# A two-layer convolution kernel: the order of work and the buffers at the opening of its second layer

## The chip, the cores and the metric

The kernel runs on one core of a Trainium2 chip. The metric is the device time of one execution in microseconds (us); the time before is the median of three runs. The engines are named as in the profile: PE is TensorE (matrix products) and PEld its weight loads, DVE is VectorE, ACT is ScalarE, POOL is GpSimd, and SP is the queue that issues all of this kernel's transfers.

## The reference

Two bottleneck layers follow one another on an input x of 64 images, 1024 channels, 14 x 14 positions, all in float32.

```python
# layer 0: 1x1 conv 1024->256, 3x3 conv 256->256, 1x1 conv 256->1024, each with batch norm
out = relu(bn(conv(x, w1) + b1)); out = relu(bn(conv(out, w2) + b2)); out = bn(conv(out, w3) + b3)
x = relu(x + softplus(residual_scale) * out)

# layer 1: 1x1 conv, deformable 3x3 conv, 1x1 conv, each with group norm (32 groups, per image)
a = relu(gn(conv(x, w1b)))                    # 256 channels
om = conv(a, w_off, pad=1) + b_off            # 27 channels: 9 x-offsets, 9 y-offsets, 9 masks
sampled[k] = bilinear(a, grid + tap k + offset k) * sigmoid(mask k)
h2 = relu(gn(einsum(sampled, w2b)))           # over 256 channels x 9 taps
out = relu(gn(conv(h2, w3b)) + x)
```

Batch norm needs statistics over all images, so no image can leave layer 0 before all have been through its third convolution. Group norm works on one image, so layer 1 goes through the images two at a time.

## The kernel before, in words

Layer 1 treats 32 pairs of images. A pair's stages are: the residual sum that ends layer 0 for it (`residual`, L212 on VectorE and a ReLU L224 on ScalarE for each of eight channel blocks); the first convolution (`first_conv`, L1072) with its statistics, norm and ReLU (`first_norm`, an object `gn1`); a transform of the result for the offset convolution (`transform`, L1136 on VectorE with an edge copy L1140 on GpSimd); the offset convolution (`offset_conv`, L1160), whose result is summed into the tile `off` by a bias on ScalarE (L1175) and eight additions on VectorE (L1176, L1177, L1187); sampling; the second convolution (`second_conv`, L1388, tile `pd`) with its norm `gn2`; the third (`third_conv`, L1500) with its norm.

Bilinear sampling is done as a matrix product (`sampling`, L1359): the transposed pixels `aT` of a pair times a matrix of weights. A weight is a product of a row factor and a column factor, each max(0, 1 - |distance|). `selection` writes `off` and the sigmoid of the masks to DRAM (tile `dm`, L1201 and L1202) and reads them back broadcast over rows (`wt` and `mk`, L1214). `factors` adds the grid (`distances`: L1224 on VectorE, then Abs and ReLU on ScalarE, L1225 and L1226), multiplies the row factor by the mask (L1231) and writes both factors to DRAM (`wd`, L1244). `spread_rows` and `spread_columns` read them back broadcast over 126 partitions: S (L1299) and X (L1321), each in three pieces for each of two sets of taps (e = 0: five taps, e = 1: four). `corners` multiplies S by X piece by piece (L1339). ScalarE then copies each sampled tile from PSUM to a buffer `sm` (L1367), 20 copies for a pair, and the second convolution reads `sm`.

To save space X lies in the buffer that later takes `sm` of the same set (`sample_buffer`, tags sm0 and sm1); the rest of the buffer sm1 takes the transform of the next pair. `transposes` makes `aT`; `lend` copies parts of it to other partitions by two transfers (L1275). `load(p)` fetches x of pair p (`load_x`, L195) and its third-convolution result of layer 0 (`load_h3`, L201).

TensorE's order is written out by hand as a list of steps (`put` places extra steps ahead of numbered ones, `weave` mixes two lists). `fill` is the opening: pairs 0, 1 and 2 go through their first stages before the loop over `slot(t)`, in which pair t is sampled and goes through its second convolution, while pair t+1 is prepared and pair t-1 finished. In the manual schedule only TensorE is bound to that order; instructions of other engines, transfers included, are placed by the scheduler, except those wrapped in `tc.keep_in_program_order`. [...]The same builder makes a second path (`FULL`) for larger offsets behind a branch.

Of the kernel before, what the change touches and what calls it, by code (L numbers as in the profile page):

```python
# [10 lines left out]
FP = mybir.dt.float32  # L11
AF = mybir.ActivationFunctionType
ALU = mybir.AluOpType
# [31 lines left out]
def kernel(  # L45
# [146 lines left out]

    def load_x(p):
        for i in range(2):
            nc.sync.dma_start(  # L195
                Y[p % 4][:, :, ts(i, HW)], x[2 * p + i].rearrange("(b p) q -> p b q", p=P)
            )

    def load_h3(p, r):
        for half in range(2):  # L200
            nc.sync.dma_start(  # L201
                r[:, ts(half, HB)].rearrange("p b q -> p (b q)"), h3[p][:, ts(half, HB * N2)]
            )
# [701 lines left out]
    def build_second_bottleneck(l1, path, run, early):  # L905
# [144 lines left out]
        def load(p):  # L1050
            start(p)
            load_x(p)
            load_h3(p, Z0)

# [163 lines left out]
        def factors(p):  # L1218
# [3 lines left out]
            def distances():  # L1222
                wt = q["wt"]
                tc.keep_in_program_order(nc.vector.tensor_tensor(wt, wt, base_sb, ALU.add))  # L1224
                nc.scalar.activation(wt, wt, AF.Abs)  # L1225
                nc.scalar.activation(wt, wt, AF.Relu, bias=1.0, scale=-1.0)  # L1226

# [40 lines left out]
        def lend(p):  # L1268

            aT = pairs[p]["aT"]  # L1270
            for j in range(1, NS - 1):
                m = (starts[0] + R - starts[j]) * W
                for k, q0, q1 in ((0, 0, m), (NS - 1, m, QR)):
                    first = (starts[j] - starts[k]) * W
                    nc.sync.dma_start(  # L1275
                        aT[q0:q1, :, :, j, :], aT[first + q0 : first + q1, :, :, k, :]
                    )
# [15 lines left out]
        def spread_rows(p, e):  # L1293

            q = pairs[p]
            k0, k1 = tapsets[e]
            S = one.tile([QR, wide * KT[e % 2]], FP, tag=f"S{e % 2}", name=f"S_{p}_{e}")
            for g, r0, piece in pieces(e):
                nc.sync.dma_start(  # L1299
                    S[:, piece],  # L1300
                    q["wd"][g][0, r0 : r0 + R, k0:k1, :]
                    .rearrange("r k n -> r (k n)")
                    .unsqueeze(1)
                    .to_broadcast([R, W, piece.stop - piece.start]),
                )
            q["S"][e] = S

        def spread_columns(p, e):
# [3 lines left out]
            n = wide * KT[e % 2]  # L1312
            if shared:
                t = sample_buffer(e, f"X_{p}_{e}")
                X = t[:QR, :n]
                if e == 1:
                    transformed[p + 1] = t[:, n:]
            else:
                X = one.tile([QR, n], FP, tag=f"X{e % 2}", name=f"X_{p}_{e}")
            for g, r0, piece in pieces(e):  # L1320
                nc.sync.dma_start(  # L1321
                    X[:, piece],
                    q["wd"][g][1, :, k0:k1, :]
# [3 lines left out]
                )  # L1327
            q["X"][e] = X

        def corners(p, e):  # L1330
# [5 lines left out]
            for g, r0, piece in pieces(e):  # L1336

                tc.keep_in_program_order(
                    nc.vector.tensor_tensor(S[:, piece], S[:, piece], X[:, piece], ALU.mult)  # L1339
                )  # L1340
# [282 lines left out]
        def slot(t):  # L1623
# [16 lines left out]
            for e in range(2, E):  # L1640
                sp[e - 2].append(lambda e=e: this and (spread_rows(t, e), spread_columns(t, e), corners(t, e)))
            d1 = part(front and not (early and t < 2), first_conv, t + 1)
            norm1, norm2, norm3 = (
                part(front, first_norm, t + 1),
                part(back, second_norm, t - 1),
# [16 lines left out]
            else:  # L1662
                extra = list(zip((3, 6, 8, 9, 10, 10, 10), norm2)) + list(zip((0, 2, 4, 4, 5, 5), norm1))
                extra = sorted(extra + [(9, w) for w in weights[1:]], key=lambda v: v[0])
# [13 lines left out]
            if ahead:  # L1678
                todo += [lambda: spread_rows(t + 1, 0), lambda: spread_columns(t + 1, 0)]
                todo += [lambda: spread_rows(t + 1, 1), lambda: lend(t + 1)]  # L1680
            if back:
# [4 lines left out]
            extra = [lambda: corners(t + 1, 0)] if t + 1 in ((1, NP - 1) if early else ()) else []  # L1686
            at = (12,)
            if t == NP - 1:

                extra, at = ends2[:-1], [len(pd[E - 1]) // 2 + n for n in (3, 5, 6, 6)]  # L1690
            todo += put(pd[E - 1], extra, at)
            if ahead:
                todo.append(lambda: spread_columns(t + 1, 1))
            for step in todo:
# [58 lines left out]
        def fill():  # L1753

            for p in range(3):
# [4 lines left out]
                first_conv(1),  # L1760
                first_norm(0) + [lambda: residual(2)] + offset_conv(0) + selection(0) + factors(0),
                (3, 6, 7, 7, 7, 7, 8) + (12,) * (MB * 3) + (12, 16, 16),
            )
            steps += [lambda: spread_rows(0, 0), lambda: spread_columns(0, 0), lambda: spread_rows(0, 1)]
            steps += transposes(0, nc.scalar.copy) + [lambda: lend(0), lambda: spread_columns(0, 1)]
            steps += put(
# [100 lines left out]
```

## Time and profile before

| | |
|---|---|
| median of three runs | 2965.86 us (2965.19 to 2966.86) |
| profiled execution | 2966.53 us, span 2964.7 us |
| PE busy | 2891.8 us, 98% of the span |
| DVE, ACT, POOL busy | 72%, 40%, 32% |
| mean granted PE clock | 0.993 |
| HBM traffic | 296.63 MB read, 116.76 MB written |

Layer 0's last product starts at about 968.5 us and layer 1's first at 970.0; pair 0's second convolution begins at 1041.34, and each later pair takes about 60.5 us. Busy time is the time of an engine's own instructions; a line of the chain of waits gives the start, the length and what the end of the program waited for at that time. In a timeline the brackets give the idle time ahead of an instruction and what ended it.

### The profile page before, as it was taken

How to read it: one execution, taken by the hardware profiler on the slowest of the kernel's cores; microseconds unless marked ns; L12 is line 12 of the kernel's file. 1: busy time of each engine (PE TensorE's matmuls, PEld its weight loads, DVE VectorE, ACT ScalarE, POOL GpSimd, SP SyncE). 2: the span in 40 equal slices, each digit the busy share in tenths (PEclk: the TensorE clock that was granted, in tenths of full speed). 3: DMA queues.
4: the chain of work that ended last, by engine and by line, in shares of the span. 5: the costliest groups of instructions: out<-in, count | busy, mean ns of one | idle time of the engine just before them, and what ended most of it. 6: DMA issues, size and time to landing. Idle time of an engine off the chain costs nothing.

```text
span 2964.7 us, 37198 instructions
## 1 busy us (share of the span) xinstructions
PE 2891.8 (98%) x11653; PEld 1829.8 (62%) x11653; DVE 2133.3 (72%) x5682; ACT 1180.9 (40%) x2504; POOL 934.5 (32%) x1003
## 2 busy tenths in 40 slices
PE   9999899989999899999999999999999999999997
PEld 5555555545555466666666666666666666666654
DVE  7877899997887656676666666676666666666655
ACT  0000222115555434444544454444544454444443
POOL 4621466654665111222122221222122221222121
PEclk9999999999999999999999999999999999999999
DMA  7665000005655425554556445644565445644531
GB/s 226 190 174 152 15 1 1 1 34 198 220 219 196 150 75 178 172 157 142 158 175 180 140 144 178 175 151 141 162 174 176 140 146 179 175 154 139 166 126 45
DMA packets 350419, 424.17 MB, mean 143 GB/s; under 512 B 27876, under 2 KB 292612, under 8 KB 349956
## 3 DMA queue, kind: packets, MB, share of 16 engines
q1 hardware_dynamic: 350212, 421.71, 46.1%
q8 instruction: 94, 1.54, 0.2%
q14 instruction: 113, 0.93, 0.1%
HBM read 296.63 MB, written 116.76 MB: 139 GB/s over the span
## 4 chain that ended last, share of the span: by engine, by line
PE 83%; DVE 10%; DMA 2%; ACT 2%; issue 1%; SPq 1%; POOL 0%; ACTq 0%; DVEq 0%; POOLq 0%
PE pd L1388 25%; PE d L1072 11%; PE sp L1359 11%; PE c L385 10%; PE c L766 9%; PE d L1500 8%; PE c L530 6%; DVE v L516 3%; PE om L1160 2%; DVE off L1187 1%; PE tr L1261 1%; DMA X<-wd 1%; PE c L731 1%; ACT sm L1367 1%; DVE V L1507 1%
## 5 line engine op out<-in xcount | busy, mean ns | idle before, releaser
L1388 PE MATMUL pd<-sm,w2b_sb 128*128 128x392 f32 x2304 | 791.7, 494 | 0.0
L1388 PEld LDWEIGHTS pd<-sm,w2b_sb 128*128 128x128 f32 x2304 | 424.6, 190 | 267.9
L1359 PE MATMUL sp<-S,aT 126*128 126x420 f32 (+3 forms) x1536 | 493.4, 418 | 22.6 <-ACT sm L1367 12.1
L1367 ACT COPY sm<-sp 128x336 f32<-128x336 f32 (+3 forms) x640 | 285.2, 451 | 265.0 <-PE sp L1359 236.4
L1072 PE MATMUL d<-h,w1b_sb 128*128 128x392 f32 x1024 | 357.2, 498 | 0.8 <-ACT h L224 0.8
L530 PE MATMUL c<-v,u_sb 128*128 128x392 f32 x1024 | 343.3, 498 | 10.9 <-DVE bn1sh L167 8.2
L530 PEld LDWEIGHTS c<-v,u_sb 128*128 128x128 f32 x1024 | 194.7, 192 | 159.4 <-DVE v L516 11.8
L1359 PEld LDWEIGHTS sp<-S,aT 126*128 126x128 f32 x1536 | 255.1, 190 | 46.8 <-ACT sm L1367 32.8
L1072 PEld LDWEIGHTS d<-h,w1b_sb 128*128 128x128 f32 x1024 | 189.3, 190 | 126.9 <-ACT h L224 3.0
L1582 ACT ACTIVATE z<-z,gn_0sh 128x196 f32<-128x196 f32 x504 | 182.7, 445 | 149.8 <-DVE gn_0sh L1034 134.0
L516 DVE TENSOR_TENSOR v<-t 128x392 f32<-128x392 f32 x256 | 193.1, 812 | 0.0
L1339 DVE TENSOR_TENSOR S<-S,X 126x840 f32<-126x840 f32 (+1 forms) x192 | 160.8, 888 | 38.0 <-DMA X<-wd 34.3
L1500 PE MATMUL d<-h,w3b_sb 128*128 128x196 f32 x744 | 180.4, 332 | 0.0
L1574 DVE SCALAR_TENSOR_TENSOR z<-z,gn_0sc,h 128x196 f32<-128x196 f32 x504 | 178.6, 417 | 0.0
L1018 POOL TENSOR_TENSOR gn_0sc<-gn_0sc,mhalf 128x16 f32<-128x16 f32 (+3 forms) x35 | 94.8, 2709 | 236.8 <-DVE gn_0sc L1017 227.6
L1500 PEld LDWEIGHTS d<-h,w3b_sb 128*128 128x128 f32 x744 | 133.0, 189 | 50.4 <-issue 19.4
L1512 POOL TENSOR_TENSOR E<-V,E 128x196 f32<-128x196 f32 x124 | 74.1, 597 | 281.8 <-DVE V L1507 281.8
L968 DVE BATCH_NORM_STATS2 gn_0st<-z 128x6 f32<-128x196 f32 x504 | 153.3, 349 | 4.2 <-ACT z L1551 0.9
L385 PE MATMUL c<-xc,w1a_sb 128*128 128x392 f32 x384 | 149.3, 497 | 5.8 <-DMA xc<-in_x_dram 5.8
L224 ACT ACTIVATE h<-h,bn3sh 128x392 f32<-128x392 f32 x256 | 140.7, 622 | 12.6 <-DVE h L212 12.6
L212 DVE SCALAR_TENSOR_TENSOR h<-h,bn3sc,h 128x392 f32<-128x392 f32 x256 | 140.7, 623 | 0.0
L718 DVE BATCH_NORM_STATS2 st<-o 128x6 f32<-128x392 f32 x256 | 127.9, 556 | 16.1 <-ACT o L749 9.5
(821 smaller groups left out, 4380.7 us busy)
## 6 DMA issues: line engine op xcount, KB each, us to landing
xc<-in_x_dram SPq DMA_DIRECT2D x128, 392.0 KB
h<-o SPq DMA_DIRECT2D x64, 784.0 KB
h<-in_x_dram SPq DMA_DIRECT2D x64, 784.0 KB
h<-h SPq DMA_DIRECT2D x64, 784.0 KB
out_dram<-z SPq DMA_DIRECT2D x126, 392.0 KB
X<-wd SPq DMA_DIRECT2D x64, 413.4 KB
S<-wd SPq DMA_DIRECT2D x64, 413.4 KB
S<-wd SPq DMA_DIRECT2D x64, 330.8 KB
```

Source lines behind the costliest of these rows:

```text
L385: nc.tensor.matmul(acc[m], a, b, start=(j == 0), stop=(j == HB - 1))
L516: nc.vector.tensor_tensor(v[:, u].rearrange("p (i y x) -> p i y x", y=7, x=7), cols[c][:, :, i : i + 13 : 2, :], cols[c][:, :, j : j + 13 ...
L530: nc.tensor.matmul(m[u], u_sb[:, c, u, k % 4, ts(o, P)], vts[k][c][:, u], start=(c == 0), stop=(c == MB - 1),)
L766: nc.tensor.matmul(planes(acc[m]), a, b, start=start, stop=True, skip_group_check=True)
L1072: nc.tensor.matmul(q["pt"][o], w1b_sb[:, c, ts(o, P)], q["y"][:, c, :], start=(c == 0), stop=(c == CB - 1),)
L1339: nc.vector.tensor_tensor(S[:, piece], S[:, piece], X[:, piece], ALU.mult)
L1359: nc.tensor.matmul(pt[:, i], q["aT"][:, i0 + i, c, starts.index(r0), :], q["S"][e][g, r0][:, :, i0 + i, :], start=(j == 0), stop=(j == len ...
L1367: nc.scalar.copy(dst, pt.rearrange("p i k n -> p k i n"))
L1388: nc.tensor.matmul(q["pd"][o], w2b_sb[:, c, k, ts(o, P)], q["sm"][e][:, c, k - k0].rearrange("p i q -> p (i q)"), start=(k == 0 and c == 0 ...
L1500: nc.tensor.matmul(bank[:, m % 2 if m < 6 else 1], a, b, start=(m < 6), stop=True, skip_group_check=True)
L1574: nc.vector.scalar_tensor_tensor(z[:, ts(i, HW)], z[:, ts(i, HW)], n.sc[:, b, i : i + 1], q["y"][:, o, ts(i, HW)], ALU.mult, ALU.add,)
L1582: nc.scalar.activation(z[:, ts(i, HW)], z[:, ts(i, HW)], AF.Relu, bias=n.sh[:, b, i : i + 1])
```

## The change

The change has these parts.

- In `fill`, the residual sum of pair 2 moves behind the offset convolution and `selection` of pair 0. The total of pair 1's statistics is pinned ahead of it.
- For pair 0, `distances` works on the column half and then the row half of `wt`, one after the other.
- X of pair 0, first set, goes to the two buffers of tag z (which the third convolution uses later), its last piece in the second of them, no longer to sm0.
- For pair 0 the pieces of S and X are issued in turn (S, X, S, X, ...), after the transposes and `lend`; the two spreading functions become generators.
- `load` (from slot 1 on) and `lend` keep their transfers in program order. In this build that moves pair 3's x and h3 loads behind pair 1's X, and pair 0's two `lend` transfers behind `wd`.
- The mean and the root of pair 2's first norm move into pair 0's second convolution (ahead of steps 5 and 8 of its last 16), and the four ReLUs that follow go ahead of steps 0, 0, 1, 1 of the next sampling.

```diff
-    def load_x(p):
+    def load_x(p, order=lambda ins: ins):
         for i in range(2):
-            nc.sync.dma_start(
-                Y[p % 4][:, :, ts(i, HW)], x[2 * p + i].rearrange("(b p) q -> p b q", p=P)
+            order(
+                nc.sync.dma_start(
+                    Y[p % 4][:, :, ts(i, HW)], x[2 * p + i].rearrange("(b p) q -> p b q", p=P)
+                )
             )
...
         def load(p):
             start(p)
-            load_x(p)
-            load_h3(p, Z0)
+
+            load_x(p, tc.keep_in_program_order)
+            load_h3(p, Z0, tc.keep_in_program_order)
...
             def distances():
-                wt = q["wt"]
-                tc.keep_in_program_order(nc.vector.tensor_tensor(wt, wt, base_sb, ALU.add))
-                nc.scalar.activation(wt, wt, AF.Abs)
-                nc.scalar.activation(wt, wt, AF.Relu, bias=1.0, scale=-1.0)
+
+                for s in (1, 0) if early and p == 0 else (slice(0, 2),):
+                    wt, add = q["wt"][:, s], base_sb[:, s]
+                    tc.keep_in_program_order(nc.vector.tensor_tensor(wt, wt, add, ALU.add))
+                    nc.scalar.activation(wt, wt, AF.Abs)
+                    nc.scalar.activation(wt, wt, AF.Relu, bias=1.0, scale=-1.0)
...
                 for k, q0, q1 in ((0, 0, m), (NS - 1, m, QR)):
                     first = (starts[j] - starts[k]) * W
-                    nc.sync.dma_start(
-                        aT[q0:q1, :, :, j, :], aT[first + q0 : first + q1, :, :, k, :]
+                    tc.keep_in_program_order(
+                        nc.sync.dma_start(
+                            aT[q0:q1, :, :, j, :], aT[first + q0 : first + q1, :, :, k, :]
+                        )
                     )
...
             for g, r0, piece in pieces(e):
-                nc.sync.dma_start(
+                yield nc.sync.dma_start(
                     S[:, piece],
...
-            if shared:
+            if shared and p == e == 0:
+
+
+                first, second = (
+                    two.tile([P, HB, N2], FP, tag="z", name=f"X_{n}").rearrange("p b n -> p (b n)")
+                    for n in range(2)
+                )
+
+                cut = [piece for _, _, piece in pieces(e)][-1].start
+                where = lambda piece: (
+                    second[:QR, : piece.stop - cut] if piece.start == cut else first[:QR, piece]
+                )
+            elif shared:
                 t = sample_buffer(e, f"X_{p}_{e}")
-                X = t[:QR, :n]
+                where = lambda piece: t[:QR, piece]
                 if e == 1:
                     transformed[p + 1] = t[:, n:]
...
             norm1, norm2, norm3 = (
-                part(front, first_norm, t + 1),
+                part(front, first_norm, t + 1)[2 if early and t == 1 else 0 :],
...
-                extra = list(zip((3, 6, 8, 9, 10, 10, 10), norm2)) + list(zip((0, 2, 4, 4, 5, 5), norm1))
+                extra = list(zip((3, 6, 8, 9, 10, 10, 10), norm2)) + list(zip((0, 0, 1, 1), norm1))
...
             at = (12,)
+            if early and t == 0:
+
+                extra, at = first_norm(2)[:2] + extra, (5, 8) + at
...
                 first_conv(1),
-                first_norm(0) + [lambda: residual(2)] + offset_conv(0) + selection(0) + factors(0),
-                (3, 6, 7, 7, 7, 7, 8) + (12,) * (MB * 3) + (12, 16, 16),
+                first_norm(0)
+                + offset_conv(0)
+                + selection(0)
+                + [lambda: pairs[1]["gn1"].total(), lambda: residual(2)]
+                + factors(0),
+                (3, 6, 7, 7, 7, 7) + (12,) * (MB * 3) + (12, 16, 16, 16, 16),
             )
-            steps += [lambda: spread_rows(0, 0), lambda: spread_columns(0, 0), lambda: spread_rows(0, 1)]
-            steps += transposes(0, nc.scalar.copy) + [lambda: lend(0), lambda: spread_columns(0, 1)]
+            steps += transposes(0, nc.scalar.copy) + [lambda: lend(0)]
+
+            steps += [lambda e=e: list(zip(spread_rows(0, e), spread_columns(0, e))) for e in range(2)]
```

## The prediction, made before the changed kernel ran

> **What bounds the kernel now.** I read the page first (TensorE busy 98% of the span), then stretches of the second layer by the windows view, then the chain of waits and the timeline where TensorE falls short.
>
> The windows view (length, then busy us of PE, weight loads, DVE, ACT, POOL, then granted clock, DMA share, GB/s) separates the opening from a steady pair:
>
> ```profile
> 964.00:1042.00 78.00, 63.72 (x275) 33.66 (x274) 44.29 (x136) 35.51 (x73) 7.51 (x12) 0.93 0.45 143
> 1066.00:1077.00 11.00, 8.97 (x37) 4.63 (x39) 7.90 (x41) 6.08 (x14) 2.76 (x4) 1.00 0.26 93
> 1131.00:1191.50 60.50, 60.26 (x278) 40.37 (x277) 40.71 (x131) 28.81 (x64) 13.69 (x18) 1.00 0.55 167
> ```
>
> A steady pair has TensorE busy for all but 0.24 of 60.5 us: nothing is to be had there. The opening lacks 14.3 us of 78, at a clock of 0.93, and the first 11 us after it lack another 2. The change works on these two places alone, so its ceiling is some 20 us. The chain of waits through the opening (start, length, what):
>
> ```profile
> 992.54 4.31 DVE h L212 x8
> 996.88 0.37 DVE om L1176
> 999.07 4.74 DMA dm<-off
> 1004.73 1.85 DMA wt<-dm
> 1008.18 0.99 DVE wt L1224
> 1011.82 2.61 DMA wd<-wt
> 1017.65 7.91 DMA X<-wd
> 1025.65 1.05 DVE S L1339
> 1026.76 0.52 ACT sm L1367
> 1027.32 3.18 PE sp L1359 x4
> ```
>
> Pair 0's offsets wait behind eight residual sums of pair 2, then for 4.7 us until 28 KB have landed in DRAM, then go through distances, write-out and spreading before the first sampling. TensorE meanwhile (timeline, idle before in brackets; the last two lines are windows of one microsecond):
>
> ```profile
> 1012.00 2.90 PE L1072 MATMUL d<-h,w1b_sb 128*128 128x392 f32 x8
> 1021.28 3.17 PE L1359 MATMUL sp<-S,aT 126*128 126x420 f32 x4 [6.38 <-DVE S L1339]
> 1027.32 14.18 PE L1359 MATMUL sp<-S,aT 126*128 126x420 f32 x44 [2.87 <-ACT sm L1367]
> 1041.34 2.14 PE L1388 MATMUL pd<-sm,w2b_sb 128*128 128x392 f32 x6
> 1019.00:1020.00 1.00, 0.00 (x0) 0.00 (x0) 0.00 (x0) 0.00 (x0) 0.00 (x0) 1.00 0.60 203
> 1020.00:1021.00 1.00, 0.00 (x0) 0.00 (x0) 0.80 (x1) 0.00 (x0) 0.00 (x0) 0.56 0.60 241
> ```
>
> It is out of work at 1014.90; the clock falls to half at about 1020.1, after 5.2 us of idling, and comes back near 1030.2. The second gap (2.87 us) is ScalarE's: pair 0's X lies in the buffer that the copies `sm` must fill, so no copy starts until all three multiplications by X are over (1026.68). The landmark below is 1041.34, the first matrix product of pair 0's second convolution.
>
> **The change, part by part.** Times are on the clock of this trace; the two kernels' orders of instructions differ only where I say.
>
> Residual of pair 2 behind the offsets. The offset products end at 993.35 as before. ScalarE's bias (0.40) no longer queues behind three ReLUs: 993.8. VectorE's eight sums row (om to off, 996.88 to 999.03 = 2.15) then ends at 996.0, not 999.03.
>
> The DRAM bounce. Before, the load of pair 3's residual input (h3, 2 x 784 KB, L201 on SP at 994.72) ran while dm was written; that load and pair 3's x (2 x 784 KB, issued near 821 before) are now issued in program order behind pair 1's X. For pair 2 the same bounce takes from 1081.80 to the next issue at 1083.22, 1.42 us. So the weights' loads start at 997.5 (before: 1003.87). SP issues three (0.81, 0.81, 0.78); before, VectorE started 2.65 us after the second was issued: data by 1001.8.
>
> What is late next: VectorE. Its queue now holds the half-map statistics (0.63, after ScalarE's mask and copy, until 997.75), the total of gn1 (0.17), eight residual sums (4.39), then the distances in halves. The sums run 998.0 to 1002.35, the two half additions (0.97 for the whole, so about 0.5 each) to 1003.4. ScalarE's ReLUs follow the sums at 0.55 to 1003.0, then four halves of about 0.45 (0.86 a whole) to 1004.8. The column factor is written from 1004.4; the row factor needs its mask product, which stands behind pair 1's norm on VectorE.
>
> That norm is the price. Its mean chain (copy to v, 1.10 us: 1000.72 to 1001.82 before) is now queued behind sums and distances, 1003.4 to 1004.55. TensorE reaches the norm's second product, after four of the sixteen steps of pair 2's first convolution, at about 1001.7, and waits 2.9 us there; before, that product ran at 1002.60, so pair 1's norm and what follows it are 2 us later. Sixteen matmuls (5.51) to 1010.4, 48 offset products (1.16 each half) to 1012.75, eight more (2.90): TensorE is through at 1015.6, against 1014.90.
>
> Does that stall halve the clock? The row shows full clock for 5.2 us of idling. [...]
>
> Row factor and spreading. Mask product 1005.2 to 1005.77, its two write-outs issued 1005.8 to 1006.6 (before, 1011.8 to 1012.7). Spreading started 1.8 us after the last issue (1014.49), so 1008.4. The two loans aT<-aT (0.88 each on SP), formerly issued at 999.98, fill 1006.6 to 1008.4: no loss of issue, though their 252 KB go ahead of S. S and X are now issued in turn, piece by piece; SP needs twelve issues of 0.75, 9 us, faster than the transfers. The bytes are the same, 3.47 MB. Before, they flowed from 1015.4 (2.2 us after X's first issue), at 200 to 230 GB/s; the sums started 4.8 us (first piece of S and X) and 17.0 us (last) after that. With the flow from 1010.5: first piece 1015.3, third about 1020.5, last 1027.5. Bounds: the flow at the best rate seen (240 GB/s) ends a us earlier, the aT bytes ahead of it cost up to 1.2 us: 1026.4 to 1028.7.
>
> X in the output's buffer (z). First product of S and X 1015.3 to 1016.35; sampling starts at 1016.4 instead of 1021.28, at full clock, and its copies start with it: the gap of 2.87 us and two slow stretches (eight 420-column matmuls at about 0.7 instead of 0.36, 2.7 us) go. One copy of ScalarE's queue waits for pair 1's offsets (mask, 1019.7) and holds TensorE 1.5 us; the first ten tiles are done near 1025. What is late then is the second half: its X still lies in the buffer sm1, so its copies wait for the last product, 1027.5 + 0.9 = 1028.4 (two tiles are ready, then TensorE waits some 2 us). A copy of 0.44, then eight tiles (six at 0.69, two at 0.55, the rows of before) make 5.7 us: the second convolution starts at 1034.1 instead of 1041.34. **Gain 7.2 us**, bounds 5.5 to 8.5.
>
> Pair 1 to slot 1. Its distances come at a fixed step of that convolution; its dm is still behind the transfers and lands some 5 us earlier with it. X of pair 1 may be loaded only when the first 20 steps are read, as before, and 2.4 MB go ahead of its end in both orders: no change. The mean and root of pair 2's norm now sit inside the convolution, where VectorE idles 10.53 us ahead of its product at 1063.80: free, and the wait of 1.67 us at L1012 near 1069 goes. But ScalarE's queue now has ReLUs before the first copies, and copy 8 stands behind the ReLU that waits for gn2: following the queues, the offset products of pair 2 start at 1076.6 instead of 1076.92. GpSimd's queue changes by one swap: gn2's root now follows pair 2's two edge copies (0.28 each), inside this estimate. I take 0.3 us, bounds -1 and +2.
>
> Pair 3's 3.2 MB are now queued on SP between pair 1's X and pair 2's dm. Before, loads of this kind moved at 320 to 430 GB/s (996 to 1001); from 1072 they end near 1082. They are used by the sums of slot 1, near 1104. Without that cover dm is late; the weights of pair 2 are needed near 1098, so there are over 8 us of slack. Later pairs keep their order; the second path is behind a branch and has no row in the trace.
>
> Sum: 7.2 + 0.3 = 7.5 us. The profiled execution took 2966.53 (span 2964.7 and 1.8 around it), so 2959.0 for it; it stands 0.67 above the median, 2965.86, so 2958.4.
>
> **The rivals.** Second gate is no gate: the transfers, no longer mixed with dm, run at 240 GB/s and the norm's move pays its 2 us; the convolution starts near 1032 and 10 to 13 us are gained, 2953 to 2956. For it: 2.0 us idle in 1066 to 1077; against: the rate was never above 241 GB/s for long.
>
> The transfer bound keeps its date: the chain is shorter, but the waits on VectorE (residual, distances, norm) and the aT bytes eat more than I count; each us by which the row factor comes later than 1005.8 goes straight through. If it is 2 to 5 us later, 2.5 to 5.5 us are gained: 2960.4 to 2963.4, within 0.2%. For it: nine instructions now stand before the distances on VectorE.
>
> Slower: pair 3's 3.2 MB block SP in front of pair 2's dm. At the spreading rate of 215 GB/s instead of 350 they take 15 us, to 1087, and dm's weights land near 1092, still in time. It decides if they end after about 1092: then VectorE waits at pair 2's distances in order, with its norms behind them. To end up 0.2% slower it must eat the 7.5 us and 5.9 more, so an end near 1106 (34 us, under 100 GB/s); then 2972 or above. DMA had a share of 0.14 in 1077 to 1095, which speaks against.
>
> **How the numbers follow.** 0.2% is 5.9 us, about what a measurement of this kernel can tell from no change. Likeliest case (5.9 to 9 us gained) 0.46; second gate no gate 0.24; date kept 0.22; slower cases 0.08, of which 0.03 lie within 0.2%. So faster 0.70, same 0.25, slower 0.05. Predicted 2958.4; the range 2953.0 to 2963.0 takes in the bounds of both costs and most of the two milder rivals, and leaves out some 0.2.
>
> **What would show it.** Right: dm issued near 996, the weights' loads near 997.5, spreading near 1008.4, no clock of 0.5 between 1014 and 1031, sampling from about 1016.4 with copies at once, the second convolution from about 1034, a wait of near 3 us at pair 1's second norm product, and one at the first sm1 copy for the product of S and X. Wrong: an S issue after 1011, a granted clock of half after the norm's stall, pair 2's dm landing after 1090, or a second convolution later than 1036.

## The result, and the profile after

| | before | after |
|---|---|---|
| median of 17 runs each, side by side | 2965.86 us | 2959.70 us |
| lowest to highest | 2960.70 to 2967.94 | 2956.96 to 2963.30 |
| profiled execution, and its span | 2966.53, 2964.7 | 2958.59, 2956.8 |
| first product of pair 0's second convolution | 1041.34 | 1033.86 |

The changed kernel takes 0.9981 of the time before (95% interval 0.9973 to 0.9988), 6.2 us less by the medians (5.6 by the ratio); 2958.4 was predicted, in a range of 2953.0 to 2963.0. The measured gain is at the low edge of the prediction's likeliest case, 5.9 to 9 us. One term of its sum was too small, because one argument about TensorE's clock was wrong.

Absolute times differ between profiles, since layer 0 ends up to 3 us earlier or later from one to the next (the landmark d0, below, lies between 966.94 and 970.04). So from here on times are also given from a landmark inside each profile, the first product of layer 1's first convolution (d0: 970.04 before, 968.87 after). "Second convolution" means the first product of pair 0's.

| from d0, us | before | predicted | after |
|---|---|---|---|
| offsets ready | 28.99 | 26.0 | 25.88 |
| first load of the weights issued | 33.83 | 27.5 | 27.31 |
| row factor's mask product | 40.93 | 35.2 | 34.78 |
| first S issued | 44.45 | 38.4 | 38.13 |
| last product of S and X of pair 0 starts | 62.4 | 57.5 | 57.0 |
| second convolution | 71.30 | 64.06 | 64.99 |
| offset products of pair 2 | 106.88 | 99.98 | 99.98 |
| end of the span | 1994.66 | | 1987.93 |

The windows view of the same three stretches as before (length, then busy us of PE, weight loads, DVE, ACT, POOL, then granted clock, DMA share, GB/s):

```profile
964.00:1034.76 70.76, 62.69 (x272) 34.54 (x271) 43.27 (x136) 35.30 (x74) 7.30 (x12) 0.95 0.44 135
1059.00:1070.00 11.00, 9.56 (x58) 5.02 (x60) 7.83 (x30) 8.28 (x19) 3.15 (x6) 1.00 0.87 244
1124.00:1184.50 60.50, 60.26 (x278) 40.37 (x277) 40.72 (x132) 28.84 (x64) 13.75 (x17) 1.00 0.53 158
```

The opening lacks 8.1 us of TensorE where it lacked 14.3, and the steady pair is what it was. The chain of waits through the opening (start, length, what):

```profile
994.77 1.39 DMA dm<-off
998.30 2.63 DMA mk<-dm
1001.40 0.56 DVE wt L1231
1003.15 0.40 PE gn_1p L1016 x2
1003.65 0.58 DVE wt L1238
1007.00 0.79 SPq L1309
1015.79 10.03 DMA X<-wd
1025.84 0.87 DVE S L1361
1026.85 0.45 ACT sm L1389
1027.35 6.68 PE sp L1381 x20
```

The eight residual sums ahead of the offsets are gone, and the write of dm to DRAM, from its issue until it has landed, takes 1.39 us instead of 4.74. The chain still ends on the last piece of X and, as before, goes on through the copies into X's buffer: the second half's gate is where the first half's was. TensorE's timeline there (idle before in brackets):

```profile
1003.15 0.39 PE L1016 MATMUL gn_1p<-gn_1v,grp_sb 128*128 128x4 f32 x2 [0.55 <-DVE gn_1v L1011]
1014.95 2.54 PE L1381 MATMUL sp<-S,aT 126*128 126x420 f32 x6 [1.10 <-DVE S L1361]
1018.34 6.77 PE L1381 MATMUL sp<-S,aT 126*128 126x420 f32 x22 [0.84 <-ACT sm L1389]
1027.35 6.68 PE L1381 MATMUL sp<-S,aT 126*128 126x336 f32 x20 [2.24 <-ACT sm L1389]
1033.86 2.14 PE L1410 MATMUL pd<-sm,w2b_sb 128*128 128x392 f32 x6
```

The stall at pair 1's norm product is 0.55 us in this profile, not the 2.9 of the prediction (more on this below), the hold by pair 1's mask 0.84, not 1.5, and the wait for the copies into sm1 2.24, against "some 2". But the last line but one is longer than the sum allowed: 7.0 us pass from the first of those copies (1026.85) to the second convolution, where 5.7 were predicted. One-microsecond windows show why (same columns; the clock is the number after POOL's):

```profile
996.00:997.00 1.00, 0.43 (x4) 0.19 (x2) 0.97 (x5) 0.85 (x3) 0.00 (x0) 1.00 0.11 31
997.00:998.00 1.00, 0.21 (x1) 0.21 (x2) 1.00 (x3) 0.89 (x2) 0.00 (x0) 1.00 0.20 34
998.00:999.00 1.00, 1.00 (x4) 0.55 (x3) 1.00 (x3) 1.00 (x3) 0.00 (x0) 0.65 0.52 166
999.00:1000.00 1.00, 1.00 (x3) 0.68 (x4) 1.00 (x3) 1.00 (x3) 0.00 (x0) 0.50 0.74 204
1001.00:1002.00 1.00, 1.00 (x3) 0.53 (x2) 0.97 (x3) 0.99 (x3) 0.00 (x0) 0.64 0.01 3
...
1025.00:1026.00 1.00, 0.11 (x1) 0.00 (x0) 0.16 (x1) 0.00 (x0) 0.00 (x0) 1.00 0.25 94
1026.00:1027.00 1.00, 0.00 (x0) 0.00 (x0) 0.70 (x1) 0.15 (x1) 0.00 (x0) 1.00 0.00 0
1029.00:1030.00 1.00, 1.00 (x7) 1.00 (x7) 0.00 (x0) 0.54 (x2) 0.00 (x0) 0.51 0.73 204
1032.00:1033.00 1.00, 1.00 (x4) 0.48 (x2) 0.00 (x0) 0.42 (x2) 0.00 (x0) 0.78 0.00 0
```

There are two spells of half clock. A mean of 0.65 in the microsecond from 998 is 0.70 us at half, so the first begins at 998.30; 0.64 from 1001 ends it at 1001.72. In the same way the second runs from 1029.02 to 1032.44. Each lasts 3.42 us, while TensorE has work, and each follows a sparse stretch whose longest idle was 1.36 us (near 997) and 2.24 us (1025.11 to 1027.35).

### The profile page after: what moved, and what is told of

Same layout as the page of the kernel before. It is cut to its first block, busy times and chain, and to the rows that moved or that the text cites. A ratio compares the mean times of both kernels' runs of the same rounds, so it can differ in the third digit from the quotient of the medians.

```text
span 2956.8 us, 37199 instructions
## 1 busy us (share of the span) xinstructions
PE 2892.5 (98%) x11653; PEld 1831.5 (62%) x11653; DVE 2133.1 (72%) x5683; ACT 1182.2 (40%) x2506; POOL 936.5 (32%) x1003
## 4 chain that ended last, share of the span: by engine, by line
PE 84%; DVE 10%; ACT 2%; DMA 1%; issue 1%; SPq 1%; POOL 0%; ACTq 0%; DVEq 0%; POOLq 0%
PE pd L1410 25%; PE d L1077 11%; PE sp L1381 10%; PE c L389 10%; PE c L770 9%; PE d L1522 8%; PE c L534 5%; DVE v L520 3%; PE om L1165 2%; DVE off L1192 1%; PE tr L1268 1%; DMA X<-wd 1%; ACT sm L1389 1%; PE c L735 1%; DVE V L1529 1%
```

## The experiments

Two ways of reading compete. By the first, the prediction's, four things shorten the chain (order of the residual, order of the loads, halves, X in z), issuing in turn costs nothing, and the last X piece with the copies behind it sets the second convolution. By the second, the transfers set it and most parts are idle ornaments. A third question came with the trace: what the half clock costs.

How far one profile can be trusted: from the first S issue to the last product of S and X the runs below take between 17.6 us and 21.1 us for the same bytes, and no run explains that spread. Differences of a microsecond or so in the landmark of one profile are therefore weak. What is firm is what lies on one side of the transfers: S's issue before them, and the tail after them, from the start of the last product to the second convolution, as long as the last product is what sets that date.

| kernel | first S | last product | second conv. | tail | median, us | of before, 95% |
|---|---|---|---|---|---|---|
| before | 44.45 | 62.4 | 71.30 | 8.9 | 2965.86 | |
| after | 38.13 | 57.0 | 64.99 | 8.0 | 2959.70 | 0.9981 [0.9973, 0.9988] |
| u_residual_first | 42.49 | 62.3 | 68.91 | 6.6 | 2961.94 | 0.9988 [0.9981, 0.9995] |
| b_load_kept | 43.21 | 62.5 | 71.72 | 9.2 | 2964.34 | 0.9996 [0.9987, 1.0004] |
| u_load_free | 40.58 | 59.8 | 66.35 | 6.6 | 2958.24 | 0.9984 [0.9977, 0.9990] |
| u_whole | 40.01 | 60.6 | 68.57 | 8.0 | 2959.50 | 0.9986 [0.9977, 0.9995] |
| u_no_z | 38.36 | 57.3 | 66.16 | 8.8 | 2959.74 | 0.9978 [0.9969, 0.9987] |
| u_not_in_turn | 38.22 | 56.8 | 64.10 | 7.3 | 2955.25 | 0.9972 [0.9962, 0.9982] |
| u_norm2_back | 38.54 | 57.8 | 65.60 | 7.8 | 2958.87 | 0.9981 [0.9974, 0.9988] |
| n_keep_warm | 38.06 | 59.1 | 66.38 | 7.2 | 2958.22 | 0.9979 [0.9970, 0.9988] |
| n_gate_off | 37.94 | 58.3 | 62.28 | 4.0 | 2955.23 | 0.9961 [0.9947, 0.9975] |
| n_gate_off_lend | 37.56 | 55.1 | 60.85 | 5.7 | 2953.71 | 0.9964 [0.9950, 0.9978] |
| n_mask_later | 37.97 | 57.5 | 62.62 | 5.1 | 2954.02 | 0.9964 [0.9950, 0.9977] |
| n_mask_kept | 37.43 | 55.7 | 60.40 | 4.7 | 2951.83 | 0.9955 [0.9942, 0.9969] |

(Positions are from d0. The medians were measured at different times; across the table compare the ratios. The last four rows have five runs each, the others 9 to 21.)

**Is the second half's gate a gate?** n_gate_off puts the second and third piece of pair 0's second X into what is left of z, so that the copies into sm1 wait for the first product only:

```diff
 in spread_columns, shared, p == e == 0:
+    q["z"] = first, second
...
 in spread_columns, shared, p == 0, e == 1:
+    last = [piece for _, _, piece in pieces(e)]
+    spare = {last[1].start: q["z"][0][:, 1120:], last[2].start: q["z"][1][:, 840:]}
+    where = lambda piece: (
+        spare[piece.start][:QR, : piece.stop - piece.start]
+        if piece.start in spare
+        else t[:QR, piece]
+    )
```

> The changed kernel, with the second and third piece of pair 0's second X in what is left of the two z buffers, so that the copies into sm1 wait for the first product of that set alone. Landmark: from the first product of the second layer's first convolution to the first of pair 0's second convolution, 71.3 us before and 65.0 after the change. Theory (the last product of S and X holds the copies, and the low activity meanwhile brings a spell of half clock): 62.4 to 63.2 us, and no half clock after the sampling has begun. Rival (ScalarE's copies and TensorE set the pace there in any case): 64.5 or more.

```profile
1015.06 2.54 PE L1390 MATMUL sp<-S,aT 126*128 126x420 f32 x6 [2.06 <-DVE S L1370]
1018.50 12.16 PE L1390 MATMUL sp<-S,aT 126*128 126x420 f32 x42 [0.90 <-ACT sm L1398]
1030.50 2.14 PE L1419 MATMUL pd<-sm,w2b_sb 128*128 128x392 f32 x6
```

It is; the second convolution, at 62.28, is even a little under the band. From 1018.50 TensorE samples without a break. The wait of 2.24 us and the second spell of half clock are gone, and the tail falls from 8.0 to 4.0 us although X landed 1.3 us later in this run. TensorE's own work now sets the second convolution, no longer the last product, so the gate cost the changed kernel between 2.7 us (by the second convolution, 64.99 to 62.28) and 4 us (by the tail). The rival "second gate is no gate" is out. In the totals, 0.9961 against 0.9981, the intervals still touch.

**What is the half clock's part of that?** n_keep_warm leaves the gate as it is and gives TensorE something to do in front of it:

```diff
 in sampling's step:
+    if p == 0 and e == 1 and turn == 2 and early:
+        idle = ps_d.tile([P, N2], FP, tag="pd1", name="idle")
+        for _ in range(5):
+            nc.tensor.matmul(
+                idle, w2b_sb[:, 0, 0, :P],
+                q["sm"][0][:, 0, 0].rearrange("p i q -> p (i q)"), start=True, stop=True,
+            )
```

> The changed kernel with five more products of TensorE (128x392 each, w2b by a part of pair 0's sampled tile, into a bank that the second convolution overwrites later) between the second and the third tile of pair 0's second half, where TensorE otherwise idles 2.24 us waiting for the copies into sm1. They leave the gate and its wait untouched and only fill it. Theory (the 7.0 us from the first of these copies to the second convolution are 5.7 at full clock, and the rest is the half clock that follows the sparse stretch 1025 to 1028): no half clock between 1029 and 1032, first product of the second convolution 63.7 to 64.3 after the first product of the layer's first convolution (the changed kernel: 64.99), time 2958.6 to 2959.4 on the changed kernel's 2959.7. Rival A (the stage is bounded by ScalarE's copies, not by TensorE's clock): 64.8 to 65.2 with the clock full. Rival B (the drop is set by something else than TensorE's own activity): half clock again near 1029, 65.0 or later.

```profile
1025.04 3.46 PE L1380 MATMUL idle<-sm,w2b_sb 128*128 128x392 f32 x10
1028.33 5.15 PE L1391 MATMUL sp<-S,aT 126*128 126x336 f32 x20
1033.32 2.14 PE L1420 MATMUL pd<-sm,w2b_sb 128*128 128x392 f32 x6
```

```profile
1029.00:1030.00 1.00, 1.00 (x6) 0.50 (x5) 0.00 (x0) 0.78 (x2) 0.00 (x0) 1.00 0.66 190
1030.00:1031.00 1.00, 1.00 (x8) 0.91 (x7) 0.00 (x0) 0.56 (x3) 0.00 (x0) 1.00 0.54 196
1031.00:1032.00 1.00, 1.00 (x4) 0.32 (x3) 0.00 (x0) 0.64 (x2) 0.00 (x0) 1.00 0.07 16
```

The half clock near 1029 that rival B expected did not come. The same tiles take 5.0 us to the second convolution (1028.33 to 1033.32) instead of 6.5 (1027.35 to 1033.86): the spell cost 1.5 us, and ScalarE was not the bound.

That the filler kept the clock up is likely, but one profile does not show it. In the profiles with two spells their starts lie whole steps of 3.41 us apart, and these steps lie elsewhere in each profile (last section; the first spell begins 29.43 us from d0 in after, 35.07 here, at 1002.01). Without the filler these tiles could have started near 1027.6 (an estimate: 0.5 us after the first copy at 1027.10, as in after), and TensorE would have been busy for half of the step from 1025.90 to 1029.31, counted on from 1002.01; of the ten steps with 0.46 to 0.50 busy half clock followed seven.

The landmark itself, 66.38, missed what was expected, 63.7 to 64.3. X landed 2.2 us later here, after the same issue. The filler was also twice as long as meant (each 128x392 product is two matmuls in the trace, so x10 and 3.46 us) and held the tiles some 0.8 us beyond the first free bank. That half clock is what the stage lacked is shown; that filling the wait pays in the total is not.

**X in z.** u_no_z puts pair 0's first X back into the buffer that the copies fill (`if shared and p == e == 0:` made false):

> The changed kernel with pair 0's first X back in sm0. Theory: the first copies wait for the third product, near 51 us after the first product of the layer instead of 47, but what follows waits for the second set's last product in any case; with a spell of half clock the landmark (65.0 after the change) becomes 64.5 to 66, so the buffer is worth under 1 us by itself. Rival: the buffer is worth the gap and the slow stretch that it removed before, and the landmark goes to 68 or more.

The copies wait for all three products again, TensorE idles 3.92 us before its third tile, and the tail is 8.8 us. The second convolution comes 1.2 us later than after, barely above the band. The gap that z removed was real, but with the second gate still there most of what it freed was waited for again. The total, 0.9978, cannot be told from after's.

**The residual's order.** u_residual_first has the order of before at this place:

```diff
-    first_norm(0)
-    + offset_conv(0)
-    + selection(0)
-    + [lambda: pairs[1]["gn1"].total(), lambda: residual(2)]
-    + factors(0),
-    (3, 6, 7, 7, 7, 7) + (12,) * (MB * 3) + (12, 16, 16, 16, 16),
+    first_norm(0) + [lambda: residual(2)] + offset_conv(0) + selection(0) + factors(0),
+    (3, 6, 7, 7, 7, 7, 8) + (12,) * (MB * 3) + (12, 16, 16),
```

> The changed kernel with the residual sum of pair 2 back ahead of pair 0's offset convolution. Theory: off ends 3 us later, the distances and the row factor some 4 us later, so the landmark goes from 65.0 to 68 to 70. Rival (the gain comes from the loads of pair 3 that no longer sit in front of dm): 65 to 66.5.

The offsets are ready at 28.88, S is issued 4.4 us later than after, and the second convolution is 3.9 us later: within the expectation, and the largest part. The total, 0.9988, points the same way.

**The order of the loads,** taken out of after (u_load_free: `load_x(p)` and `load_h3(p, Z0)` without program order) and put into before alone (b_load_kept):

> The changed kernel with the loads of pair 3 left to the scheduler, as before. Its order puts h3 of pair 3 (2 x 784 KB) behind the weights' loads and ahead of the write-out of the factors. Theory: 1.6 MB go through the engines just as the factors are written and S starts, landmark 66.5 to 68.5 instead of 65.0. Rival (the order of the loads matters only for dm, which is ahead of them here): 65.

> The kernel before with one part of the change alone: the loads of pair 3 (x and h3) in program order, behind pair 1's X. Theory: dm lands in 1.4 us instead of 4.7, but the distances and the mask product stand behind pair 1's transform on VectorE and start little earlier: landmark 70.3 to 71.3 (before: 71.3). Rival: the 3.3 us of the bounce come through whole: 68.

Both second convolutions land just outside the theory's bands (66.35 under 66.5, 71.72 over 71.3) and nearer to them than to the rivals, 65 and 68. In u_load_free the distance to the rival is no more than the transfers' spread, so S has to decide. There the write-out of the factors meets pair 3's load, where in before the write-out of dm met it. The factors' write-out took 2.61 us in before; the chain of waits of u_load_free has

```profile
1002.90 5.33 DMA wd<-wt
```

and S is issued 2.4 us later; in after S follows the last write-out by 2.0 us, which the loans of aT fill. So the 1.6 MB collided with the write of dm in the one order and with that of the factors in the other, and holding them back is worth about 2.4 us at S. At the second convolution only 1.4 are left, since TensorE waited less afterwards (tail 6.6). In before alone the same order brings the weights' loads 1.3 us and S 1.2 us forward, and nothing comes of it: last product 62.5, second convolution 71.72. The copies' gate and 10.2 us of half clock lie behind it. The totals do not contradict: 0.9984 and 0.9996, the one near after and the other near before.

**The halves.** u_whole does the distances and both activations on the two factors at once:

```diff
-    for s in (1, 0) if early and p == 0 else (slice(0, 2),):
+    for s in (slice(0, 2),):
```

> The changed kernel with pair 0's distances and their two activations on both factors at once, as in the kernel before. Theory (the halves bring the column factor's write-out forward by about 1 us, but the row factor's mask product and the loads of X behind it are hardly touched, and S and X flow together): first product of the second convolution 65.0 to 66.0 after the first product of the layer's first convolution (the changed kernel: 64.99), first issue of S 0.5 to 1.2 us later than 38.13, time 2959.7 to 2960.7. Rival (the halves are worth their full share of the chain, or the later start avoids the half clock): above 66.2, or below 64.7.

The rival came out. The mask product starts 1.9 us later than after (36.72 against 34.78), as does S (40.01). The reason is its place in VectorE's order. After, in the first fence, and u_whole, in the second:

```profile
1003.57 0.16 DVE L1021 TENSOR_SCALAR gn_1sc<-gn_1p 128x4 f32<-128x4 f32 x1 [0.48 <-PE gn_1p L1016]
1003.65 0.57 DVE L1238 TENSOR_TENSOR wt<-wt,mk 126x392 f32<-126x392 f32 x1
```

```profile
1003.08 0.16 DVE L1021 TENSOR_SCALAR gn_1sc<-gn_1p 128x4 f32<-128x4 f32 x1 [0.56 <-PE gn_1p L1016]
1004.36 0.23 DVE L1028 TENSOR_TENSOR gn_1sc<-gn_1sc,vec 128x2 f32<-128x2 f32 x2 [1.12 <-POOL gn_1sc L1022]
1004.63 0.16 DVE L1031 TENSOR_TENSOR gn_1sh<-gn_1gm,gn_1sc 128x4 f32<-128x4 f32 x1
1004.71 0.57 DVE L1238 TENSOR_TENSOR wt<-wt,mk 126x392 f32<-126x392 f32 x1
```

With whole factors the mask product falls behind three of the norm's instructions (two in the line with x2), which wait for GpSimd's root. The halves are worth the difference in the queue, not the shorter instructions. The other 1.7 us of the 3.6 at the second convolution came with the transfers, and that part is inside their spread. The total, 0.9986, fits a loss of one or two us and also none.

**S and X in turn.** u_not_in_turn issues all pieces of S, then all of X, as before:

```diff
-    steps += [lambda e=e: list(zip(spread_rows(0, e), spread_columns(0, e))) for e in range(2)]
+    steps += [lambda e=e, f=f: list(f(0, e)) for e in range(2) for f in (spread_rows, spread_columns)]
```

> The changed kernel with all pieces of S ahead of all pieces of X for each set. Theory (the last product of S and X decides): the first product comes some 2.5 us later, but the last one at the same time: landmark 65 to 65.8. Rival (the start of sampling decides): 67 or more.

```profile
1016.21 15.77 PE L1381 MATMUL sp<-S,aT 126*128 126x420 f32 x48 [3.43 <-DVE S L1361]
1031.81 2.14 PE L1410 MATMUL pd<-sm,w2b_sb 128*128 128x392 f32 x6
```

Neither expectation held: undoing it lost nothing. Sampling starts 2.4 us later and then runs without a break, with one spell of half clock inside it, and ends at 64.10. The early start that issuing in turn buys is spent waiting at the second gate. That it even gains is not shown, as 0.9 us lies within the transfers' spread and 0.9972 overlaps with 0.9981.

**Pair 2's norm.** u_norm2_back returns its mean and root to where before had them, in slot 1's sampling:

```diff
-    part(front, first_norm, t + 1)[2 if early and t == 1 else 0 :],
+    part(front, first_norm, t + 1),
...
-    extra = list(zip((3, 6, 8, 9, 10, 10, 10), norm2)) + list(zip((0, 0, 1, 1), norm1))
+    extra = list(zip((3, 6, 8, 9, 10, 10, 10), norm2)) + list(zip((0, 2, 4, 4, 5, 5), norm1))
...
-    extra, at = first_norm(2)[:2] + extra, (5, 8) + at
```

> The changed kernel with pair 2's first norm back in the sampling of pair 1. Landmark unchanged (65.0). From the layer's first product to the offset products of pair 2: 106.9 us before, 100.0 after the change. Theory (ScalarE's queue takes back most of what the norm's move gives): 100.4 to 101.2. Rival (the wait of 1.7 us at the norm comes back whole): 101.6 or more.

```profile
1063.10 0.39 PE L1016 MATMUL gn_2p<-gn_2v,grp_sb 128*128 128x4 f32 x2 [1.89 <-DVE gn_2v L1011]
1072.00 2.11 PE L1165 MATMUL om<-X,woff_sb 128*32 128x196 f32 x48
```

The rival came out. From the second convolution to pair 2's offset products it takes 37.18 us; after takes 34.99 and before 35.58. The norm's second product waits 1.89 us, the copies behind it wait too, and a further spell of half clock lies at 94.5 to 97.9 (ten products of sampling took 3.09 us there, in after 2.32). So the move was worth 2.2 us between these two profiles, of which that spell, 3.4 us at half clock, can be up to 1.7 (an estimate: half its length), while the prediction, counting from before, gave the slot 0.3 (it measured 0.59). Both are right: in the earlier order the shortened opening would have lost 1.6 us here (37.18 against 35.58), and the move prevents that. In the total, 0.9981, the 2.2 us can't be seen.

**A better version.** n_gate_off_lend adds to n_gate_off that the transposes and the loans aT<-aT that follow them come earlier. The loans are then issued before the factors' write-outs and no longer stand between these and S:

```diff
     + selection(0)
-    + [lambda: pairs[1]["gn1"].total(), lambda: residual(2)]
+    + transposes(0, nc.scalar.copy)
+    + [lambda: pairs[1]["gn1"].total(), lambda: residual(2), lambda: lend(0)]
     + factors(0),
...
-    steps += transposes(0, nc.scalar.copy) + [lambda: lend(0)]
```

> The kernel of the opened second gate, with the two loans of aT issued between the loads of the weights and the write-out of the factors, where SP is idle for some 4 us. Theory (the transfers of S and X set the date of everything behind): 252 KB less ahead of S, and the first X may start before the row factor has landed: the last product comes 1 to 1.5 us earlier, landmark 61.3 to 62.3 us. Rival (TensorE's own work after the norm of pair 1 sets the start of sampling): 62.4 to 63.2 as without it.

The second convolution comes at 60.85, somewhat earlier than the band, and the total is within its spread the same as n_gate_off's. TensorE is now the limit at the start, and the next wait shows: the third tile waits 2.02 us for ScalarE, whose queue has pair 1's sigmoid ahead of the first copies, itself waiting for pair 1's offsets (ScalarE stood idle for 4.44 us ahead of it).

```profile
1013.58 1.57 PE L1390 MATMUL sp<-S,aT 126*128 126x420 f32 x4
1017.18 12.69 PE L1390 MATMUL sp<-S,aT 126*128 126x420 f32 x44 [2.02 <-ACT sm L1398]
```

n_mask_later moves `selection(1)` (the sigmoid, the bounce and the weights' loads of pair 1) from the end of pair 2's first convolution behind the fourth tile of sampling:

> The version with both the second gate away and the loans of aT issued early, in which pair 1's mask, its DRAM bounce and its weights' loads are also moved from the end of pair 2's first convolution into pair 0's sampling, behind its fourth tile, so that ScalarE's queue no longer holds a sigmoid that waits for pair 1's offsets ahead of the first copies. Theory (of the 2.02 us that TensorE waited there 1.4 to 2 are the sigmoid's): wait of at most 0.9 us, second convolution 58.9 to 59.8 after the first product of the layer's first convolution (60.85 with the mask ahead), and the same gain at the offset products of pair 2 (96.68 before), time 2952.3 to 2953.2. Rival A (the S and X pieces are late then: TensorE waits for VectorE's products instead): 60.3 to 61. Rival B (pair 1's weights, now issued later, come late for its distances): the second convolution early, but the offset products of pair 2 not before 96.5.

The wait was 1.74 us: ScalarE's order, which the program's scheduler decides, still had the sigmoid first. So this run tells nothing on the question. n_mask_kept holds the first four copies and that sigmoid in the order written (`tc.keep_in_program_order`):

> In the version named n_mask_later the order that the program writes for ScalarE was still decided by the scheduler, which put pair 1's sigmoid ahead of the first copies again (1016.80, before the copies at 1017.60), so that run tested nothing. Here the first four copies and the sigmoid are held in the order written: copies first. Theory (the wait of about 2 us of TensorE at its third tile is the sigmoid's): wait of at most 0.9 us, and the second convolution 13.9 to 14.9 us after the start of the first sampling tile instead of 16.1 (n_gate_off_lend) and 15.8; time 2952.5 to 2953.4, if S and X arrive as in n_gate_off_lend. Rival (TensorE then catches up with VectorE's products of S and X, which become the limit): the wait moves to a later tile, 15.2 to 16 us, time 2953.5 to 2954.5.

```profile
1014.02 14.33 PE L1392 MATMUL sp<-S,aT 126*128 126x420 f32 x48
1028.19 2.14 PE L1423 MATMUL pd<-sm,w2b_sb 128*128 128x392 f32 x6
```

```profile
1014.92 0.51 ACT L1400 COPY sm<-sp 128x420 f32<-128x420 f32 x1 [0.22 <-PE sp L1392]
1017.61 0.53 ACT L1204 ACTIVATE mask<-off 32x392 f32<-32x392 f32 x1
```

The whole sampling of pair 0 now runs in one piece, with no wait shown before it or inside: 14.2 us to the second convolution, inside the expectation, and the rival is out. It takes 2951.83 us (0.7 below the lower end expected), 0.9955 of before [0.9942, 0.9969], and beats both kernels; its interval lies wholly below after's.

## Why the prediction was right, and which term was not

- **Residual and bounce:** offsets at 26.0 predicted, 25.88 measured; weights' loads at 27.5 and 27.31. The 1.42 us of pair 2's bounce was the right row: 1.39 us. That the early order of pair 3's loads matters is shown by u_load_free.
- **VectorE's queue and the norm:** mask product and S came 0.4 and 0.2 us earlier than predicted, and the norm as late as predicted (34.28; predicted 34.56, from 1004.6). In after TensorE waits only 0.55 us for it, because the first spell of half clock stretched the products ahead until they filled the wait (eight took 4.73 us, where eight at full clock, from 1010.95, took 2.90). Where the spell came behind the norm, the wait is near the predicted 2.9: u_no_z has

```profile
1002.64 0.40 PE L1016 MATMUL gn_1p<-gn_1v,grp_sb 128*128 128x4 f32 x2 [2.47 <-DVE gn_1v L1011]
```

  and half clock from 1002.88; u_whole, n_keep_warm, n_mask_later and n_mask_kept wait 2.07 to 2.59 us, with half clock within 1.2 us behind. So the stall cost more than the predicted wait: in these five profiles half clock came on top of it, and TensorE is through with the opening's convolutions at 46.4 to 46.9 (by the prediction 45.56), where those with the earlier spell are at 44.7 to 45.4. That after was spared this is luck: its spell began at 29.43 from d0, ahead of the stall, and that of u_no_z, with the same order of work there, at 34.74, behind it. In n_mask_kept it did cost: its first product of S and X was ready at 44.7, and sampling started at 46.23.
- **Transfers:** last product at 57.5 predicted, 57.0 measured. The spread over the runs (17.6 to 21.1 us from first S issue) says that so close a hit is partly luck, and with it that of the total.
- **The mis-sized term** is the last stage, "a copy of 0.44, then eight tiles ... 5.7 us". It measured 7.0. The copies started 0.4 us earlier than predicted and the stage was 1.3 longer, which gives the whole miss at the second convolution: 64.06 - 0.4 + 1.3 = 65.0. The prediction had argued on the clock that "The row shows full clock for 5.2 us of idling". The row says only when the clock fell in that one gap. In after, half clock followed on 1.36 and 2.24 us of idling, inside a stretch of sparse work. The two spells start 30.72 us apart (998.30, 1029.02), nine times 3.41 us; each lasts 3.42, and TensorE was busy for 0.49 of the 3.41 us ahead of each (last section). The prediction applied a clock argument to the norm's stall and none to the wait at the second gate, which it had itself put at some 2 us. n_keep_warm puts a price on that: 1.5 us.
- **Slot 1:** 0.3 predicted, 0.59 measured, which made up for part of the miss. The 6.90 us at pair 2's offset products are 6.73 at the end of the span. The profiled executions differ by 7.9, of which 1.2 are layer 0's end.
- **The slower rival:** pair 3's loads of 3.2 MB, ahead of pair 2's dm in the queue, were over near 1075 (292 to 442 GB/s in slices of 0.6 us from 1066 to 1073), and pair 2's weights were asked for at 1076.1, far ahead of the 1092 at which the prediction put the danger. The bounce took 2.5 us there instead of 1.4, but pair 3's first convolution starts 78.35 us after the second convolution of pair 0, against 78.94 before, so nothing was lost by it.

What stays open: why the spreading transfers take between 17.6 and 21.1 us for the same bytes, and whether issuing in turn is worth anything once the second gate is gone, as no run has n_gate_off's buffers with the old issue order.

## What to carry to other kernels

When a buffer that a stage writes is still read by the step ahead of it, freeing the first half of the stage only moves the wait to the second half: follow the gate through every half and price it there, clock included. Read the price of a move from the order on the engine's queue after the change, not from the length of the moved instructions: the halves were worth three places in VectorE's queue, and the norm's move prevented a loss that the profile of before did not yet show. Do not call a wait free because the clock survived a longer one elsewhere: here full clock lasted through 5.2 us of idling in before, and half clock followed on 1.36 and 2.24 us in after. One profile does not settle it either: the same order of work met half clock ahead of the norm's stall in after (29.43 from d0) and behind it in u_no_z (34.74).

## What the hardware showed that was not expected

- Spells of half clock came in whole steps, 3.42 us in after, 6.82 in u_residual_first and 10.24 us in before (1020.12 to 1030.36 by the same working, where the prediction read 1030.2; three steps), and in the seven profiles with two spells between 966 and 1061 us their starts lie two to nine whole steps of 3.41 us apart. Counted off in such steps from a spell, these are four stretches at full clock, two of before and two of after (length, busy us of PE, weight loads, DVE, ACT, POOL, clock, DMA share, GB/s):

```profile
1013.29:1016.70 3.41, 1.61 (x5) 0.57 (x3) 2.69 (x11) 0.89 (x2) 0.00 (x0) 1.00 0.42 109
1016.70:1020.12 3.42, 0.00 (x0) 0.00 (x0) 0.00 (x0) 0.00 (x0) 0.00 (x0) 1.00 0.57 215
994.89:998.30 3.41, 1.68 (x11) 1.00 (x10) 3.00 (x8) 3.15 (x9) 0.00 (x0) 1.00 0.18 42
1025.61:1029.02 3.41, 1.67 (x7) 0.99 (x7) 0.86 (x1) 1.46 (x4) 0.00 (x0) 1.00 0.32 71
```

  The first left the clock as it was; half clock followed on each of the others. So the 5.2 us of idling in before were the end of a step that had begun busy and one idle step. Counted in this way in all 14 profiles, over 960 to 1075 us, there are 434 steps at full clock. Half clock followed all 15 in which TensorE was busy for less than 0.46 of the time, seven of the ten between 0.46 and 0.50, and none of the 409 above 0.51. What sets the clock these profiles do not show.
- 28 KB took 4.74 us to land in DRAM beside a load of 1.6 MB and 1.39 us without it; the factors' write-out took 5.33 us beside such a load, in u_load_free, and 2.61 in before.
